# One-hot operands made two batches ahead instead of one, in a graph network's count building

## The chip, the core and the metric

The kernel runs on one core of a Trainium2 chip. The metric is the device time of one execution in microseconds (us). Five engines work side by side, each through its own instructions in their program order, and wait for each other by semaphores: PE (TensorE, matrix products; its weight loads are shown as an engine of their own, PEld), DVE (VectorE), ACT (ScalarE), POOL (GpSimd, which here asks for rows by indirect transfers) and SP (SyncE, which only starts transfers).

## What is computed

The reference normalises x (6250 nodes by 256 channels), and then runs four layers of a graph network over 100000 edges that are sorted by destination. A layer adds to each node the sum of its neighbours' rows and puts the result through a small network of three matrices:

```python
h = jnp.maximum(_layernorm(x, axis=-1), 0.0)
def agg(h):
    return jax.ops.segment_sum(h[src], dst, num_segments=N)
for l in range(NL - 1):
    h = x + agg(x)
    h = jax.nn.relu(h @ W1s[l] + b1s[l])
    h = jax.nn.relu(h @ W2s[l] + b2s[l])
    x = h @ W3s[l] + b3s[l]
h = x + agg(x)
h = jax.nn.relu(h @ cW1 + cb1)
h = jax.nn.relu(h @ cW2 + cb2)
return h @ cW3 + cb3
```

The result is x plus what this returns. All of it is float32.

## The kernel before

The 6250 nodes are 49 blocks of 128. For 31 of them the neighbour sum is a dense product: a matrix of edge counts (how many edges go from each of the 6250 sources to each of the 128 destinations of the block, uint8) times the node rows. For the others the rows are gathered by indirect transfers on POOL (L1427) and summed with matmuls against a small one-hot (`hot`, L1450; matmuls L1466; the sum is added to the node's own row by L1486 and L1495).

**Building the counts.** The count matrices are made once, during the first layer, by the generator `build` (L1092 to L1131). A block is two halves of 64 destinations. A half is 16 groups of 4 destinations, each with up to 128 edges that lie on the partitions. A batch is 4 groups. For a batch DVE writes two one-hot tiles in bf16: `lo`, 128 edges by 4x128 (which of the 128 rows of a source block), and `hi`, 128 edges by 4x196 (which of 49 source blocks and which of 4 destinations). Both come from L1073, called by `low_hot` and `high_hot`; each kind has two buffers. A matmul of `lo` by `hi` (L1114, 196 columns) gives the counts of one group in PSUM. Two groups share a PSUM tile `bp` (three buffers), and are converted to uint8 into `at`: the first pair of a batch by ACT (L1122), the second by DVE (L1124). In the first 24 steps (a step is one pair, two steps are a batch) ACT does both. When a block is whole, DVE adds the identity (L1128, the node's own row) and SP stores the matrix (L1129) for the later layers. `pair` (L1068, ACT) spreads the indices of a half for DVE; it is made one half ahead.

**What runs around it.** In the first layer PE goes through units: a unit is up to 4 matmuls of 512 columns (L1642) of a node block's product, whose left side `a` ACT converts from uint8 (L1602). Before each unit, `tick` issues what has come due: `un` (L1654, the product's two halves added), the MLP of finished blocks (L1526 transposes, L1276 and L1333 matmuls, `zz` at L1341), the gathered sums (L1466). Then `product_by_node` takes steps from `build` until a goal for this unit is reached: in most units one batch, in about one in four none, now and then one and a half. Then come the unit's own matmuls. Ahead of all that, 12 batches are built back to back (L1760 to L1765).

All engines run their instructions in the order in which these calls are made (`manual_schedule`, L1001). On DVE the order around batch k is: what `tick` issued before it, `lo` of k+1, `hi` of k+1, the conversion of k's second pair (L1124); if a block has ended, L1128.

Of the kernel before, what the change touches and what calls it, by code (L numbers as in the profile page):

```python
# [396 lines left out]
def sorted_edges(  # L397
# [55 lines left out]
    BATCH = 4  # L453
# [547 lines left out]
    with tc.manual_schedule():  # L1001
# [61 lines left out]
        def pair(hots, k):  # L1063

            if k < len(batches):
                s = batches[k][0]
                pairs[s] = hots.tile([P, 2, GSUB, 2], BF16, name="pairs", bufs=3)
                nc.scalar.copy(pairs[s], clT[:, :, :, s - S0, None].to_broadcast([P, 2, GSUB, 2]))  # L1068

        def one_hot(o, values, which, n):  # L1070

            shape = [P, BATCH, n // 2, 2]
            nc.vector.tensor_tensor(  # L1073
                o.rearrange("p q (n t) -> p q n t", t=2),
                values.rearrange("p (n t) -> p n t", t=2)[:, None, :, :].to_broadcast(shape),
                which[:, :, None, :].to_broadcast(shape), OP.is_equal)

        def low_hot(hots, k):
            if k < len(batches):
                s, q0 = batches[k]  # L1080
                lo = hots.tile([P, BATCH, P], BF16, name="lo", bufs=2)
                one_hot(lo, lanes, pairs[s][:, 1, q0:q0 + BATCH, :], P)
                hot[k] = [lo]

        def high_hot(hots, k):
            if k < len(batches):
                s, q0 = batches[k]
                hi = hots.tile([P, BATCH, HW], BF16, name="hi", bufs=2)
                one_hot(hi, cols, pairs[s][:, 0, q0:q0 + BATCH, :], HW)
                hot[k].append(hi)  # L1090

        def build(hots, ats, ps_b):  # L1092


            each = GSUB // BATCH
            pair(hots, 0)
            low_hot(hots, 0)
            high_hot(hots, 0)
            step = 0
            for k, (s, q0) in enumerate(batches):  # L1100
                b, half = divmod(s, 2)
                if half == 0 and q0 == 0:
                    at = counts[b] = ats.tile([P, NT, P], U8, name="at", bufs=3)
                lo, hi = hot.pop(k)
                if q0 == 0:
                    pair(hots, k + each)
                for q in range(0, BATCH, 2):
                    if q == 0:
                        low_hot(hots, k + 1)
                    elif q == 2:  # L1110
                        high_hot(hots, k + 1)
                    bp = ps_b.tile([P, W], F32, name="bp")
                    for m in range(2):
                        mm = nc.tensor.matmul(bp[:, m * HW:(m + 1) * HW], lo[:, q + m, :],  # L1114
                                              hi[:, q + m, :], start=True, stop=True)
                    passed(BUILD, mm)
                    d = half * 64 + (q0 + q) * GD
                    o = at[:, :, d:d + 2 * GD].rearrange("p h (i d) -> p h i d", i=2)
                    v = bp[:, :2 * HW].rearrange("p (i h d) -> p h i d", i=2, d=GD)
                    step += 1  # L1120
                    if step % 2 or step <= 2 * PRE:
                        nc.scalar.copy(o, v)  # L1122
                    else:
                        nc.vector.tensor_copy(o, v)  # L1124
                    if half and q0 + q + 2 == GSUB:
                        p, i = place_of[b]
                        own = at[:, b, :]
                        nc.vector.tensor_tensor(own, own, ident, OP.add)  # L1128
                        nc.sync.dma_start(out=mats[p][:, :, i, :],  # L1129
                                          in_=at.rearrange("p (k h) d -> p k (h d)", h=CH))  # L1130
                    yield  # L1131
# [449 lines left out]
        def passed(t, ins=None):  # L1581

            clock[0] += t
            if ins is not None:
                paced[:] = [ins.ins.name]
                for g in layers:
                    g.flow()
# [160 lines left out]
        with tc.tile_pool(name="hots", bufs=1) as hots, tc.tile_pool(  # L1748
            name="ats", bufs=1
        ) as ats, tc.tile_pool(name="rings", bufs=AHEAD + 2) as rings, tc.tile_pool(  # L1750
            name="gath", bufs=24
        ) as gath, tc.tile_pool(
            name="ps_a", bufs=2, space=PSUM
        ) as ps_a, tc.tile_pool(name="ps_b", bufs=3, space=PSUM) as ps_b:
            begun = {0: clock[0]}
            rings.tile([P, 192], U8, name="align", bufs=1)
            layers[0].begin()
            layers[0].send(8)
            beside = build(hots, ats, ps_b)
            while now[0] < PRE:  # L1760
                for _ in range(2):
                    next(beside)
                    built[0] += 1
                tick(layers[0])
                layers[0].advance()  # L1765
            later(1, lambda: later(2, lambda bad=verdict(): judge(bad)))
            for team in teams:
                product_of_team(*team, ps_a, beside, team == teams[-1])
            assert next(beside, None) is None and built[0] == total
# [73 lines left out]
```

## Time and profile before

| | us |
|---|---|
| median of 3 runs | 2105.08 (2103.89 to 2105.66) |
| the profiled execution | 2104.15 |
| its span, first to last instruction | 2102.4 |
| counts built (first to last L1114) | 116.6 to 638.0 |

| engine | busy us | share of the span |
|---|---|---|
| PE | 2031.7 | 97% |
| PEld | 1501.4 | 71% |
| POOL | 1441.1 | 69% |
| DVE | 933.8 | 44% |
| ACT | 879.7 | 42% |

In the profile's groups of instructions the number after the bar is the busy time, then the mean duration of one, then the idle time of that engine just before them and what ended it. In the view of waits a row is "who waits, for whom: total us, times, longest". A timeline row begins with the start and the duration in us; the bracket is the idle time before it and what ended it. Durations of neighbours on one engine overlap a little, so the step from start to start is what an instruction costs in a full queue.

### The profile page before, as it was taken

How to read it: one execution, taken by the hardware profiler on the slowest of the kernel's cores; microseconds unless marked ns; L12 is line 12 of the kernel's file. 1: busy time of each engine (PE TensorE's matmuls, PEld its weight loads, DVE VectorE, ACT ScalarE, POOL GpSimd, SP SyncE). 2: the span in 40 equal slices, each digit the busy share in tenths (PEclk: the TensorE clock that was granted, in tenths of full speed). 3: DMA queues.
4: the chain of work that ended last, by engine and by line, in shares of the span. 5: the costliest groups of instructions: out<-in, count | busy, mean ns of one | idle time of the engine just before them, and what ended most of it. 6: DMA issues, size and time to landing. Idle time of an engine off the chain costs nothing. (4 is left out here: it accounts for less than half of the span.)

```text
span 2102.4 us, 33308 instructions
## 1 busy us (share of the span) xinstructions
PE 2031.7 (97%) x12117; PEld 1501.4 (71%) x12117; DVE 933.8 (44%) x2108; ACT 879.7 (42%) x1799; POOL 1441.1 (69%) x1450
## 2 busy tenths in 40 slices
PE   6889999999999999999999999999999999999997
PEld 4667666666667777777777777777777777777775
DVE  5987767767673422222233322222224333333333
ACT  5866656556555523322333432323333433323331
POOL 3747777777774377777777377777777377777773
PEclk9999999999999999999999999999999999999999
DMA  5544545545554654545556555555456455656554
GB/s 166 171 136 137 158 150 154 157 150 153 155 153 145 212 163 146 169 152 179 155 174 196 186 165 149 172 159 179 147 171 202 161 179 156 196 174 206 169 171 129
DMA packets 184324, 346.92 MB, mean 165 GB/s; under 512 B 32030, under 2 KB 118080, under 8 KB 184150
## 3 DMA queue, kind: packets, MB, share of 16 engines
q0 software_dynamic: 68144, 183.13, 29.9%
q1 hardware_dynamic: 114078, 159.72, 23.1%
q8 instruction: 97, 1.59, 0.3%
q10 hardware_dynamic: 1928, 1.85, 0.3%
q14 instruction: 77, 0.63, 0.1%
HBM read 286.50 MB, written 58.07 MB: 164 GB/s over the span
## 5 line engine op out<-in xcount | busy, mean ns | idle before, releaser
L1427 POOL DMA_INDIRECT rows<-table,idx x1377 | 1381.2, 1003 | 587.5 <-issue 225.4
L1720 PE MATMUL agg<-a,XY 128*128 128x512 f32 x4116 | 976.6, 394 | 1.9 <-DVE clT L1654 1.9
L1720 PEld LDWEIGHTS agg<-a,XY 128*128 128x128 f32 x4116 | 765.2, 188 | 190.1 <-issue 32.4
L1618 ACT CAST a<-at 128x512 fp32r<-128x512 uint8 (+1 forms) x549 | 332.7, 616 | 633.2 <-PE agg L1720 591.3
L1618 DVE CAST a<-at 128x512 fp32r<-128x512 uint8 (+1 forms) x550 | 251.0, 458 | 522.4 <-PE agg L1720 476.0
L1642 PE MATMUL agg<-XY,a 128*128 128x512 f32 x1519 | 420.9, 410 | 1.7 <-ACT a L1602 1.0
L1642 PEld LDWEIGHTS agg<-XY,a 128*128 128x128 f32 x1519 | 268.3, 189 | 54.2 <-issue 9.2
L1466 PE MATMUL sums<-rows,hot 128*32 128x256 f32 x3726 | 233.4, 381 | 8.7 <-DMA rows<-table,idx 8.5
L1122 ACT CAST at<-bp 128x392 uint8<-128x392 f32 x260 | 125.0, 489 | 188.8 <-PE bp L1114 182.6
L1466 PEld LDWEIGHTS sums<-rows,hot 128*32 128x32 f32 x3726 | 118.5, 109 | 117.1 <-issue 27.6
L1602 ACT CAST a<-at 128x512 fp32r<-128x512 uint8 (+2 forms) x362 | 197.5, 575 | 4.7 <-PE agg L1642 4.7
L1124 DVE CAST at<-bp 128x392 uint8<-128x392 f32 x236 | 132.8, 563 | 133.5 <-PE bp L1114 132.7
L1495 DVE TENSOR_TENSOR u<-u,sums 128x256 f32<-128x256 f32 x81 | 33.9, 419 | 265.3 <-PE agg L1720 241.9
L1114 PE MATMUL bp<-hi,lo 128*128 128x196 bf16 x992 | 129.5, 251 | 16.9 <-DVE hi L1073 16.1
L1073 DVE TENSOR_TENSOR hi<-cols,pairs 128x784 bf16<-128x784 bf16 x248 | 139.1, 561 | 0.0
L1333 PE MATMUL ps<-w,h 128*128 128x256 f32 x588 | 135.1, 382 | 1.4 <-ACT h L1279 0.9
L1276 PE MATMUL ps<-h,w 128*128 128x512 f32 (+3 forms) x332 | 133.7, 545 | 2.0 <-DVE zz L1317 1.7
L1114 PEld LDWEIGHTS <-lo 128*128 128x128 bf16 x992 | 72.8, 98 | 87.7 <-DVE hi L1073 37.3
L1333 PEld LDWEIGHTS ps<-w,h 128*128 128x128 f32 x588 | 112.4, 192 | 18.7 <-ACT h L1279 1.3
L1073 DVE TENSOR_TENSOR lo<-lanes,pairs 128x512 bf16<-128x512 bf16 x248 | 103.6, 418 | 0.2 <-issue 0.2
L1530 ACT ACTIVATE h<-ps,bias 128x256 f32<-128x256 f32 (+1 forms) x116 | 47.5, 464 | 134.1 <-PE ps L1526 134.1
L1341 DVE TENSOR_TENSOR zz<-ps,w 128x512 f32<-128x512 f32 (+1 forms) x75 | 50.2, 678 | 117.1 <-PE ps L1333 117.1
(173 smaller groups left out, 959.0 us busy)
## 6 DMA issues: line engine op xcount, KB each, us to landing
at<-mat SPq DMA_DIRECT2D x152, 448.0 KB
mat<-at SPq DMA_DIRECT2D x31, 784.0 KB
rows<-table,idx POOLq DMA_INDIRECT x1377
table<-zz SPq DMA_DIRECT2D x72, 256.0 KB
back<-table SPq DMA_DIRECT2D x99, 128.0 KB
xs<-in_x_dram SPq DMA_DIRECT2D x8, 768.0 KB
table<-zs SPq DMA_DIRECT2D x12, 512.0 KB
out_dram<-zz SPq DMA_DIRECT2D x24, 256.0 KB
```

What stands on the lines that cost most here:

```text
L1073: nc.vector.tensor_tensor(o.rearrange("p q (n t) -> p q n t", t=2), values.rearrange("p (n t) -> p n t", t=2)[:, None, :, :].to_broadcast( ...
L1114: mm = nc.tensor.matmul(bp[:, m * HW:(m + 1) * HW], lo[:, q + m, :], hi[:, q + m, :], start=True, stop=True)
L1122: nc.scalar.copy(o, v)
L1124: nc.vector.tensor_copy(o, v)
L1276: mm = nc.tensor.matmul(ps[:mp, :w], weights[l][0][:, c, i * P:i * P + mp], h1[:, c, :w], start=(c == 0), stop=(c == KC - 1))
L1333: mm = nc.tensor.matmul(o, h2[0][:, c, nodes], w3[:, c, :], start=(c == 0), stop=(c == KC - 1))
L1427: got = nc.gpsimd.indirect_dma_start(out=t, out_offset=None, in_=tables[self.l][:, :], in_offset=bass.IndirectOffsetOnAxis(ap=idx[:, o:o + ...
L1466: nc.tensor.matmul(self.sums[m * Q:(m + 1) * Q, :C], self.hot[:, c - min(rounds), m, :], self.rows[g, c + 4 * m], start=(c == ROUNDS[0][0] ...
L1602: nc.scalar.copy(a[:, i * m * P:(i + 1) * m * P].rearrange("p (j d) -> p j d", j=m), counts[b][:, j:j + m, :])
L1618: cast(o, at[:, :, d:d + m * P])
L1642: mm = nc.tensor.matmul(agg, a[:, d:d + P], XY[:, j, :], start=(j == 0), stop=(j == NT - 1))
L1720: mm = nc.tensor.matmul(agg[c][:, :w], XY[:, j, o:o + P], a[:, :w], start=(at == 0 and half == 0), stop=(at == NT - 1 and half == 1))
```

## The change

The first two one-hots of each kind are made ahead of the loop. In the loop, the making of `lo` and `hi` for the next batch is taken from the places ahead of the two pairs of a batch; in its stead both one-hots for the batch after the next are made behind the conversion of the second pair, when the batch has been used up. Buffers, operations and their number stay.

```diff
             each = GSUB // BATCH
             pair(hots, 0)
-            low_hot(hots, 0)
-            high_hot(hots, 0)
+            for k in range(2):
+                low_hot(hots, k)
+                high_hot(hots, k)
             step = 0
...
                 for q in range(0, BATCH, 2):
-                    if q == 0:
-                        low_hot(hots, k + 1)
-                    elif q == 2:
-                        high_hot(hots, k + 1)
                     bp = ps_b.tile([P, W], F32, name="bp")
...
                         nc.scalar.copy(o, v)
                     else:
                         nc.vector.tensor_copy(o, v)
+                    if q + 2 == BATCH:
+                        low_hot(hots, k + 2)
+                        high_hot(hots, k + 2)
                     if half and q0 + q + 2 == GSUB:
                         p, i = place_of[b]
                         own = at[:, b, :]
```

## Prediction

> **What bounds the kernel now.** I read the page first, then the waits of the weight loads in the stretch in which counts are built, then timelines at the longest waits.
>
> ```profile
> span 2102.4 us, 33308 instructions
> PE 2031.7 (97%) x12117; PEld 1501.4 (71%) x12117; DVE 933.8 (44%) x2108; ACT 879.7 (42%) x1799; POOL 1441.1 (69%) x1450
> ...
> L1114 PE MATMUL bp<-hi,lo 128*128 128x196 bf16 x992 | 129.5, 251 | 16.9 <-DVE hi L1073 16.1
> L1073 DVE TENSOR_TENSOR hi<-cols,pairs 128x784 bf16<-128x784 bf16 x248 | 139.1, 561 | 0.0
> ```
>
> PE is the bound. The largest idle time ahead of any group of its matmuls is that of the counting matmuls, 16.9 us, of which 16.1 wait for `hi`. That is what the change can touch, and the shown idle time is not all of it, since a matmul's end is modelled. The weight loads tell it better:
>
> ```profile
> 127.00:640.00 513.00, 499.10 (x3388) 351.37 (x3387) 371.44 (x843) 307.97 (x695) 369.70 (x366) 0.99 0.50 149
> ```
>
> ```profile
> PEld L1114 <- DVE hi L1073: 31.4, 60, 1.5
> PEld L1114 <- DVE at L1124: 18.6, 68, 0.3
> ...
> PEld L1114 <- DVE zz L1341: 0.5, 2, 0.3
> ```
>
> The first row is the stretch of 513 us: busy time and instructions of PE, PEld, DVE, ACT and POOL. A load ahead of a batch idles 0.27 us even where nothing is late (18.6/68), while the product's matmuls ahead of it run out. The 60 loads that waited for `hi` idle 31.4, so 31.4 - 60x0.27 = 15.2 us are lost there. Batch by batch, counting the excess over 0.27 of the late ones, I get 15.4 in 28 waits. Before 127 us, in the 12 batches that are built back to back:
>
> ```profile
> PE bp L1114 <- DVE hi L1073: 4.5, 11, 1.1
> ```
>
> **What the change does to the order.** Call X what DVE has to do between the conversion of batch k and the first one-hot of k+2. Before, DVE's order is: conversion k, X, `lo` k+2, `hi` k+2, conversion k+1. After, it is: conversion k, `lo` k+2, `hi` k+2, X, conversion k+1. The one-hots pass X, and nothing else moves: each conversion has the same work ahead of it as before. Where X is empty, nothing changes. The new place needs no new wait: the buffers of k are free when k's last matmul has ended, and the conversion just ahead has waited for that matmul. (With half batches `lo` and `hi` both move ahead too.) X is `hot`, `un`, `zz`, `u`, L1128: 0.2 to 1.7 us.
>
> **A wait that goes whole.**
>
> ```profile
> 278.80 0.57 DVE L1124 CAST at<-bp 128x392 uint8<-128x392 f32 x1 [6.90 <-PE bp L1114]
> 279.46 0.29 DVE L1128 TENSOR_TENSOR at<-at,ident 128x128 uint8<-128x128 uint8 x1
> 279.67 1.28 DVE L1341 TENSOR_TENSOR zz<-ps,w 128x512 f32<-128x512 f32 x2
> 280.87 0.41 DVE L1495 TENSOR_TENSOR u<-u,sums 128x256 f32<-128x256 f32 x1
> 281.20 0.42 DVE L1073 TENSOR_TENSOR lo<-lanes,pairs 128x512 bf16<-128x512 bf16 x1
> 281.54 0.56 DVE L1073 TENSOR_TENSOR hi<-cols,pairs 128x784 bf16<-128x784 bf16 x1
> ```
>
> ```profile
> 282.15 0.11 PEld L1114 LDWEIGHTS <-lo 128*128 128x128 bf16 x2 [1.40 <-DVE hi L1073]
> ```
>
> DVE had idled 6.90 us, and when the matmuls of a batch let it go, X (1.74 us, 279.46 to 281.20) stood ahead of the one-hots. PE lost 1.40 - 0.27 = 1.13. With the one-hots directly behind the conversion (which holds DVE some 0.48 us, 278.80 to 279.28), `hi` ends at 279.28 + 0.34 + 0.56 = 280.18; the load could go at 282.15 - 1.13 = 281.02. Nothing is lost there, and an MLP on PE follows, so the 1.13 us stay.
>
> **A wait that only moves on.**
>
> ```profile
> 513.93 0.56 DVE L1124 CAST at<-bp 128x392 uint8<-128x392 f32 x1
> 514.60 0.29 DVE L1128 TENSOR_TENSOR at<-at,ident 128x128 uint8<-128x128 uint8 x1
> 514.81 0.95 DVE L1450 TENSOR_TENSOR hot<-colf,rel 128x768 f32<-128x768 f32 x1
> 515.68 0.41 DVE L1654 TENSOR_TENSOR un<-un,agg 128x256 f32<-128x256 f32 x1
> 516.01 0.42 DVE L1073 TENSOR_TENSOR lo<-lanes,pairs 128x512 bf16<-128x512 bf16 x1
> 516.35 0.56 DVE L1073 TENSOR_TENSOR hi<-cols,pairs 128x784 bf16<-128x784 bf16 x1
> 516.82 0.56 DVE L1124 CAST at<-bp 128x392 uint8<-128x392 f32 x1
> 517.30 0.42 DVE L1073 TENSOR_TENSOR lo<-lanes,pairs 128x512 bf16<-128x512 bf16 x1
> ```
>
> ```profile
> 516.96 0.28 PEld L1114 LDWEIGHTS <-lo 128*128 128x128 bf16 x4 [1.21 <-DVE hi L1073]
> 518.27 0.28 PEld L1114 LDWEIGHTS <-lo 128*128 128x128 bf16 x4 [0.27 <-DVE hi L1073]
> ```
>
> A unit with a batch takes PE 1.31 us (516.96 to 518.27), and DVE needs 0.81 for the two one-hots (516.01 to 516.82) and 0.48 for a conversion: 1.29. In such a run DVE has no slack, so X is a debt. The wait here is 1.21 - 0.27 = 0.94. After the change `hi` is ready at 514.41 + 0.90 = 515.31, and the batch goes at 516.96 - 0.94 = 516.02. But then X (0.21 + 0.87 + 0.33 = 1.41) runs from 515.22 to 516.63, the conversion to 517.11, and the next `hi` ends at 518.01, while PE wants it at 516.02 + 1.31 = 517.33. With 0.06 from `hi` to load PE waits 0.74: only 0.20 of 0.94 is kept. A debt is paid off only where PE has something else: a unit without a batch, the MLP, a gathered sum.
>
> **The sum.** So for each wait: what is kept is the wait, less what the same DVE work makes later batches of the cluster late. I went through DVE's 843 instructions of the stretch in this way, with steps from start to start, each conversion 0.56 us behind its batch's first load at the earliest. In the order of before this gives 14.9 us of waits (the trace: 15.4), so it holds to 0.6. In the new order 4.9 are left. By cluster, start of each, wait now > left:
>
> - go whole: 211 (0.23), 282 (1.13), 328 (0.24), 355 (0.55), 375 (0.56), 408 (0.44), 440 (0.34), 444 (0.56), 561 (0.62), 608 (1.40), 630 (0.48): 6.5 > 0
> - go in part: 165 (1.04 > 0.35), 262 (0.90 > 0.44), 314 (1.14 > 0.55), 421 (0.81 > 0.41), 517 (0.94 > 0.76), 579 (2.26 > 0.54): 7.1 > 3.05
> - stays: 494 (1.71 > 1.76); the last 0.1 is at 199.
>
> Kept: 14.9 - 4.9 = 10.0 by the walk, 10.5 against the trace's waits; I take 10.0.
>
> At the start, 11 waits: ten are 0.3, because a batch there takes PE 0.51 and DVE 0.81, with no X between; they stay. The eleventh has one:
>
> ```profile
> 123.57 0.29 DVE L1128 TENSOR_TENSOR at<-at,ident 128x128 uint8<-128x128 uint8 x1 [0.54 <-ACT at L1122]
> ```
>
> ```profile
> 124.73 0.51 PE L1114 MATMUL bp<-hi,lo 128*128 128x196 bf16 x4 [1.13 <-DVE hi L1073]
> ```
>
> ```profile
> 125.11 2.66 ACT L1122 CAST at<-bp 128x392 uint8<-128x392 f32 x6 [0.66 <-PE bp L1114]
> ```
>
> Here `lo` stood behind L1128, which waited 0.54 for ACT. The one-hots pass it, and PE goes on. But ACT, which does all conversions here and then the first `a` for which PE waits, idled only 0.66 of it, so between 0 and 0.66 comes through; I take 0.6, as nothing else holds ACT there.
>
> **What is moved back.** X starts up to 0.81 us later. In the stretch no load except those of L1114 waited for X (`zz`: 0.5 us in 2, the usual 0.27 each), and what reads it comes units later: a table store, a transpose, the next gathered sum. L1128 only holds up SP's store and casts of a block whose units come later. I take 0; the bound is 134 pieces of X (the stretch's `hot`, `un`, `zz`, `u` and L1128) by 0.81 = 109 us if PE always waited at once for X, and not below 0. ACT, POOL and SP issue what they did.
>
> Against its own time: 2104.15 - 10.0 - 0.6 = 2093.55. That execution was 0.93 below the median; on the median's scale 2105.08 - 10.6 = **2094.5**.
>
> **The rivals.**
>
> *All of it comes back.* If DVE finds room for X in idle time that my walk doesn't see, all goes: 15.4 + 0.7 = 16.1, so 2089.0. For: DVE is busy 371 of 513 us. Against: the run at 517, where it has 0.02 per batch to spare.
>
> *DVE is the bound in the clusters*, and waits mostly move on, as at 517, where 0.20 of 0.94 stays: 15.4 x 0.21 = 3.3, so 2101.8, inside what can be told from no change (0.2%, about 4 us for this kernel). For: the cluster at 494. Against: most long waits come after DVE has idled, with MLP work on PE behind.
>
> *It does nothing*: if X were mostly recorded behind the one-hots already, the time stays, 2105. Against: the two timelines.
>
> *Slower: the gathers.* POOL builds its indirect transfers beside the one-hots:
>
> ```profile
> L1427 POOL DMA_INDIRECT rows<-table,idx x8: 957/1180/1320, 115.8 to 126.1; - x8
> ```
>
> ```profile
> L1427 POOL DMA_INDIRECT rows<-table,idx x366: 947/953/1850, 126.1 to 639.0; - x183
> ```
>
> ```profile
> POOL rows L1427 <- PE bp L1114: 41.4, 91, 2.8
> POOL rows L1427 <- PE agg L1642: 37.0, 68, 10.0
> ```
>
> Where one-hots run back to back a gather takes 1.18 us (median), over the stretch mostly 0.95 (mean 369.70/366 = 1.01). POOL's slack is what it waits for PE: 78.4 in 159 waits, less some 0.3 each that is there anyway, 31 us. If the new places put every gather beside a one-hot, 366 x 0.17 = 62 us come on, 31 beyond the slack; PE would wait for rows from a mean of 1.01 + 31/366 = 1.09 us on, and the time would be 2105.08 - 10.6 + 31 = 2125. Against: there are as many one-hots as before, in almost the same places. The Trainium skill, "SBUF — State Buffer", section "Who interferes with whom", says that a VectorE operation with two SBUF inputs contends with GpSimd's reads through a shared port, and that issue order decides who blocks. The trace agrees as far as 0.95 against 1.18 goes; by that rule the loss could as well fall on DVE, but the one-hots take 0.42 and 0.56 everywhere, so here it is POOL that stretches.
>
> **How the numbers follow.** The forecast has 0.66, all of it 0.15, DVE the bound 0.10, nothing 0.03, the gathers 0.06. Range: from 2088 (all of it, less 1 for the scatter between runs of +-0.9) to 2102 (DVE the bound); left out are the last two and some of the edges. The likeliest alone: 2092 to 2097. Faster by over 0.2%: 0.66 + 0.15 and a little of the third, 0.82; within: 0.12; slower: 0.06.
>
> **What would show it.** In the changed profile L1073's pair follows L1124 directly; at the place of the 282 us wait the load of L1114 has no excess; the waits of L1114's loads for `hi` in the stretch have an excess near 5 us, most in the run near 494 and its like; the last L1114 ends near 627 in place of 638, and the layers after it take as long as before. Wrong would be: an excess over 10 us; new waits of PE for `zz`, `u`, `un` or `hot`; a gather mean above 1.09 with L1466 waiting for rows; or a gain in the first layer that a later stage gives back.

## The result and the profile after

The changed kernel took 2092.72 us (median of 4 runs, 2091.27 to 2094.35), the kernel before 2105.37 in the same sessions: a ratio of 0.9943, 95% interval 0.9930 to 0.9957, 12.65 us less. The forecast was 2094.5, with 2088 to 2102 as its range. The profiled execution took 2093.95 with a span of 2092.2; its counting matmuls have moved from L1114 to L1111, and DVE's conversion from L1124 to L1121, by the lines that the change took out.

From the page of the changed kernel:

```profile
span 2092.2 us, 33309 instructions
PE 2032.2 (97%) x12117; PEld 1504.3 (72%) x12117; DVE 931.1 (45%) x2108; ACT 880.3 (42%) x1799; POOL 1445.3 (69%) x1450
...
L1111 PE MATMUL bp<-hi,lo 128*128 128x196 bf16 x992 | 132.0, 254 | 6.5 <-DVE hi L1073 5.7
```

DVE makes as many instructions as before (2108), and the busy times of PE, DVE and ACT differ by less than 3 us; the idle time ahead of the counting matmuls is 6.5 us in place of 16.9. The waits of the weight loads, from 127 to 640 us:

```profile
PEld L1111 <- DVE at L1121: 20.0, 73, 0.3
PEld L1111 <- DVE hi L1073: 18.6, 50, 1.4
...
PEld L1111 <- DVE at L1128: 1.3, 5, 0.3
PEld L1111 <- DVE zz L1341: 0.8, 3, 0.3
```

For `hi`, 18.6 us in 50 waits, less 0.27 each, is 5.1 lost, where it was 15.2. Below, "excess" means the same, load by load: idle time over 0.27 us, summed over the loads of the 13th batch and later that idled over 0.30 for a one-hot. It is 15.6 us in 29 loads before, and 5.6 in 13 after. The waits that end with X (`zz`, L1128) are no longer than the usual 0.27.

The place of the 1.13 us wait, first DVE and then the loads:

```profile
277.62 0.57 DVE L1121 CAST at<-bp 128x392 uint8<-128x392 f32 x1 [6.89 <-PE bp L1111]
278.10 0.41 DVE L1073 TENSOR_TENSOR lo<-lanes,pairs 128x512 bf16<-128x512 bf16 x1
278.43 0.56 DVE L1073 TENSOR_TENSOR hi<-cols,pairs 128x784 bf16<-128x784 bf16 x1
278.91 0.28 DVE L1128 TENSOR_TENSOR at<-at,ident 128x128 uint8<-128x128 uint8 x1
279.11 1.28 DVE L1341 TENSOR_TENSOR zz<-ps,w 128x512 f32<-128x512 f32 x2
```

```profile
279.29 0.46 PEld L1111 LDWEIGHTS <-lo 128*128 128x128 bf16 x6 [0.26 <-DVE at L1128]
```

The pair stands directly behind the conversion, X behind it, and the load is not late. The row merges the four loads of one batch and the first two of the next, the late ones of before, which now follow without a gap. The place where a wait only moves on, DVE's X and then the loads:

```profile
509.85 0.95 DVE L1450 TENSOR_TENSOR hot<-colf,rel 128x768 f32<-128x768 f32 x1
510.72 0.41 DVE L1654 TENSOR_TENSOR un<-un,agg 128x256 f32<-128x256 f32 x1
511.05 0.56 DVE L1121 CAST at<-bp 128x392 uint8<-128x392 f32 x1
511.53 0.41 DVE L1073 TENSOR_TENSOR lo<-lanes,pairs 128x512 bf16<-128x512 bf16 x1
511.86 0.56 DVE L1073 TENSOR_TENSOR hi<-cols,pairs 128x784 bf16<-128x784 bf16 x1
```

```profile
510.44 0.29 PEld L1111 LDWEIGHTS <-lo 128*128 128x128 bf16 x4 [0.28 <-issue]
512.47 0.28 PEld L1111 LDWEIGHTS <-lo 128*128 128x128 bf16 x4 [0.99 <-DVE hi L1073]
```

The batch at 510.44 is in time, and the next one idles 0.99, an excess of 0.72 where 0.74 was worked out.

**Where the 10.2 us of span went.** The loads of the counting matmuls, in the kernel before and the changed one:

```profile
L1114 PEld LDWEIGHTS <-lo x992: 95/98/152, 116.2 to 637.9; 128*128 128x128 bf16 x199
```

```profile
L1111 PEld LDWEIGHTS <-lo x992: 95/98/152, 116.2 to 628.7; 128*128 128x128 bf16 x199
```

They start at the same time and end 9.2 us earlier. The other 1.0 is no part of the change: 1.6 came with a dip of TensorE's granted clock (0.91 on the mean of 680 to 700 us), which of these two executions only the one of before has, and 0.8 was lost again near 2001, where rows for a gathered sum came late.

### The profile page after: what moved, and what is told of

It is laid out like the page before. It is cut to its first block, busy times and chain, and to the rows that moved or that the text cites. A ratio compares the mean times of both kernels' runs of the same rounds, so it can differ in the third digit from the quotient of the medians.

```text
span 2092.2 us, 33309 instructions
## 1 busy us (share of the span) xinstructions
PE 2032.2 (97%) x12117; PEld 1504.3 (72%) x12117; DVE 931.1 (45%) x2108; ACT 880.3 (42%) x1799; POOL 1445.3 (69%) x1450
## 3 DMA queue, kind: packets, MB, share of 16 engines
q10 hardware_dynamic: 1928, 1.85, 0.3%
## 5 line engine op out<-in xcount | busy, mean ns | idle before, releaser
L1642 PE MATMUL agg<-XY,a 128*128 128x512 f32 x1519 | 421.0, 410 | 1.7 <-ACT a L1602 1.0
L1642 PEld LDWEIGHTS agg<-XY,a 128*128 128x128 f32 x1519 | 268.3, 189 | 54.1 <-issue 9.2
L1121 DVE CAST at<-bp 128x392 uint8<-128x392 f32 x236 | 133.2, 565 | 134.6 <-PE bp L1111 133.8
L1111 PE MATMUL bp<-hi,lo 128*128 128x196 bf16 x992 | 132.0, 254 | 6.5 <-DVE hi L1073 5.7
L1111 PEld LDWEIGHTS <-lo 128*128 128x128 bf16 x992 | 74.0, 99 | 76.9 <-issue 24.5
```

Source lines behind the costliest of these rows:

```text
L1642: mm = nc.tensor.matmul(agg, a[:, d:d + P], XY[:, j, :], start=(j == 0), stop=(j == NT - 1))
```

## The experiments

Each is set against the kernel before of its own session: 2103.45 us for `hi` alone, the two with `hot` twice and the changed kernel with ACT; 2103.69 for the two with 21 row buffers, the one ahead and the first from batch 12; 2104.02 for the last four rows. "Walk" is the excess that the prediction's way through DVE's rows gives for each order.

| kernel | median us | against before | excess us (loads) | walk us |
|---|---|---|---|---|
| before | 2105.37 | | 15.6 (29) | 14.9 |
| changed | 2092.72 | -12.65 | 5.6 (13) | 4.9 |
| only `hi` two ahead | 2098.46 | -5.0 | 12.8 (23) | 12.1 |
| before, `hot` twice | 2118.48 | +15.0 | 30.6 (34) | 28.0 |
| changed, `hot` twice | 2104.71 | +1.3 | 16.0 (23) | 14.3 |
| changed, ACT converts 3 of 4 | 2086.98 | -16.5 | 1.4 (4) | 1.1 |
| changed, 21 row buffers | 2095.19 | -8.5 | 5.5 (13) | |
| three ahead, 21 row buffers | 2089.18 | -14.5 | 0.0 | 0.0 |
| one ahead, behind the conversion | 2207.9 | +104.2 | 113.7 (156) | 116.1 |
| changed from batch 12 on | 2095.88 | -7.8 | 5.5 (13) | |
| changed, again | 2091.27 | -12.75 | 5.5 (13) | 4.9 |
| changed from batch 12 on, again | 2094.39 | -9.6 | 5.5 (13) | |
| before, ACT converts 3 of 4 | 2099.04 | -5.0 | 10.9 (23) | 9.0 |
| three ahead, ACT converts 3 of 4 | 2089.85 | -14.2 | 0.0 | 0.4 |

**Only one of the two operands.**

```diff
             low_hot(hots, 0)
-            high_hot(hots, 0)
+            for k in range(2):
+                high_hot(hots, k)
...
                     if q == 0:
                         low_hot(hots, k + 1)
-                    elif q == 2:
-                        high_hot(hots, k + 1)
...
+                    if q + 2 == BATCH:
+                        high_hot(hots, k + 2)
```

> Edit: only the hi one-hot is made two batches ahead behind the conversion; lo keeps its place of before, ahead of the next batch and behind X. Theory (the pair passes X, and PE needs both): lo still stands behind X, so only the 0.48 us that hi takes is gained at a late batch and most of it becomes a wait further on; going through the DVE rows of before in this order leaves 12.1 us of 14.9 us of waits, a gain of 2.8 us over before, 2102.6 us, and the loads now wait for lo in place of hi. Rival (the late operand is hi, as the profile names it in 60 waits against 13 for lo): nearly the whole gain of the change, 10 to 12.6 us, 2093 to 2095 us.

Ratio 0.9979 (0.9969 to 0.9990). The excess falls by 2.8 us as the theory has it; the time, by the ratio, by 4.4 (2.1 to 6.5), an interval that holds the theory's 2.8 and not the rival's 10. The loads from 127 to 640 us:

```profile
PEld L1113 <- DVE lo L1073: 26.7, 52, 1.5
```

The profile now names `lo`. It had named `hi` only because `hi` came last: both stood behind X.

**X made longer, in both kernels.**

```diff
-                nc.vector.tensor_tensor(
-                    self.hot,
+                for _ in range(2 if self.l == 0 else 1):
+                    nc.vector.tensor_tensor(
+                        self.hot,
...
```

> Edit: in the kernel before, DVE writes the small one-hot of the gathered sums (hot, a piece of X, 0.87 us of DVE) twice in the first layer, 21 or so more instructions. Theory (X stands ahead of the one-hots and a late batch is lost PE time): 13.2 us slower than before, 2118.6 us, by the same walk through the DVE rows. Rival (DVE has idle time enough, 142 of 513 us, and X hides in it): under 3 us slower. Rival (DVE is the bound of the stage): the whole 21 x 0.87 = 18.3 us, 2123.7 us.

> Edit: the same doubled hot in the changed kernel. Theory: the one-hots pass X, but X remains a debt in runs of batches without slack: 9.4 us slower than the changed kernel, 2102.1 us, less than the same edit costs in the kernel before (13.2). Rival (with the change X is off the path): under 3 us. Rival (DVE is the bound of the stage): 18.3 us, 2111.0 us.

The same DVE work costs the kernel before 15.0 us (ratio 1.0073, 1.0056 to 1.0090) and the changed one 12.0 against its 2092.72, or 13.4 against the 2091.27 of a later session. By excess, which is not blurred by the scatter between runs, it is 15.0 and 10.5. Loads of before and of the changed kernel with the longer X, from 127 to 640 us:

```profile
PEld L1114 <- DVE hi L1073: 46.6, 64, 2.5
```

```profile
PEld L1111 <- DVE hi L1073: 32.1, 61, 2.4
```

So X is on the path in both, and the change makes it cheaper, not free. The 3 us of work that hides is far outside. The 18.3 us of a stage bound by DVE alone is told apart by the excess (15.0 and 10.5); the time of the kernel before alone, with 11.8 to 18.9 us as its interval, would leave room for it. The walk had 13.2 and 9.4: the sign and the order right, both 1 to 2 us low by the excess.

**DVE relieved, with the change and without.** The same one-line edit was put into both kernels:

```diff
-                    if step % 2 or step <= 2 * PRE:
+                    if step % 4 or step <= 2 * PRE:
                         nc.scalar.copy(o, v)
```

> Edit: the changed kernel with ACT converting three of four pairs instead of two, so DVE has 0.48 us less in every second batch. Theory (what is left, 5.5 us of excess at 13 loads, is DVE without slack in runs of batches): 3.7 us faster than the changed kernel, 2089.0 us, excess about 1 us. Rival (what is left is the distance of two batches, not DVE's rate): no change, 2092.7 us. Rival (ACT, 313 us busy of 513 and in order with the casts for PE, becomes late): slower than 2095 us with PE waiting for a.

> Edit: the kernel before with ACT converting three of four pairs; the one-hots stay behind X. Theory (two causes that add: X stands ahead of the one-hots, and DVE has no slack to pay it off; relief of DVE alone leaves the first): 5.9 us faster than the kernel before, about 9 us of excess left at the loads, against 1.4 us left with both edits. Rival (DVE's rate is the whole cause): all 15 us gone, 2089 us, as with both edits.

With the change it is 2086.98 (ratio to before 0.9920, 0.9903 to 0.9937), the fastest kernel of all here: 5.7 us below the changed kernel, or 4.3 below the 2091.27 of its later session, where 3.7 was expected. Without the change it gains 5.0 (ratio 0.9975, 0.9966 to 0.9984), where 5.9 was expected. The loads of the two:

```profile
PEld L1111 <- DVE lo L1073: 13.5, 50, 0.3
PEld L1111 <- DVE hi L1073: 9.1, 30, 1.0
```

```profile
PEld L1114 <- DVE hi L1073: 25.0, 53, 1.5
```

The excess tells the two causes apart: 15.6 as it was, 10.9 with DVE relieved, 5.6 with the one-hots ahead of X, 1.4 with both. ACT did not become late: PE waited once for `a`, 1.2 us, as in the changed kernel (1.0).

**More distance.** A third buffer of each kind needs 2592 bytes of every partition (4x128 and 4x196 values of 2 bytes). Three row buffers of 1 KB each are given up for it, so 21 are left, in a control too.

```diff
-            name="gath", bufs=24
+            name="gath", bufs=21
```

> Edit: the changed kernel with 21 row buffers for the gathers of the first layer instead of 24, to make room for the next run; its control. Theory and rivals: a visit takes 17 rows, and 4 more can be asked for ahead, so within 1.5 us of the changed kernel, 2092.7 us; if rows come late PE waits for them at L1466 and it is slower by the sum of those waits.

The control came out 2.5 us above the changed kernel, more than the 1.5 expected, at the same excess for one-hots. Fewer row buffers do bring waits for rows. The loads of the gathered sums from 127 to 640 us, in the changed kernel and in the control:

```profile
PEld sums L1466 <- DMA rows<-table,idx: 2.1, 5, 0.8
```

```profile
PEld sums L1466 <- DMA rows<-table,idx: 4.2, 5, 1.4
```

That is 2.1 us more, about the size of the difference, in one execution of each. The next kernel is set against this control.

```diff
-                lo = hots.tile([P, BATCH, P], BF16, name="lo", bufs=2)
+                lo = hots.tile([P, BATCH, P], BF16, name="lo", bufs=3)
...
-                hi = hots.tile([P, BATCH, HW], BF16, name="hi", bufs=2)
+                hi = hots.tile([P, BATCH, HW], BF16, name="hi", bufs=3)
...
-            for k in range(2):
+            for k in range(3):
...
-                        low_hot(hots, k + 2)
-                        high_hot(hots, k + 2)
+                        low_hot(hots, k + 3)
+                        high_hot(hots, k + 3)
```

> Edit: the control with three buffers of each one-hot, made three batches ahead. Theory (the waits left in the changed kernel are debts of X that come due one or two batches later, and a batch more of distance lets them be paid where PE has other work): the walk through the DVE rows leaves 0.0 of 4.9 us of waits, so 4.9 us faster than the control, about 2087.8 us. Rival (DVE's rate is the bound in these runs, distance doesn't help): the time of the control, excess about 5.5 us as in the changed kernel.

The third batch removes the whole excess and 6.0 us of the control's time (2089.18 against 2095.19; the times lie at 2088.82 to 2096.13 and 2094.36 to 2097.0). So in the runs without slack distance does help: DVE finds room later, when PE is at an MLP or a gathered sum. Its profiled execution, at 2096.13 the slowest of its four, waited still longer for rows (6.2 us at these loads), once like this:

```profile
316.67 1.70 PE L1466 MATMUL sums<-rows,hot 128*32 128x256 f32 x25 [1.76 <-DMA rows<-table,idx]
```

**Both remedies together.** The last two edits in one kernel.

> Edit: three buffers and three batches ahead (21 row buffers for the gathers) with ACT converting three of four pairs. Theory: nearly no wait for one-hots is left in either edit alone, so together no more than each: excess under 0.5 us, 2086 to 2089 us. Rival (they add): 2082 us. Rival (fewer row buffers bring waits for rows): slower than 2090 us with those waits at L1466.

They don't add: ratio 0.9935 (0.9921 to 0.9948), and no excess, of which three batches ahead alone had left none. At 2089.85 us it lies just above the 2086 to 2089 expected, and above the kernel that only relieves DVE (2086.98). That kernel has 24 row buffers, and the 21 show here again: the waits for rows with both remedies, and with ACT's alone:

```profile
PEld sums L1466 <- DMA rows<-table,idx: 6.1, 8, 1.7
```

```profile
PEld sums L1466 <- DMA rows<-table,idx: 1.1, 4, 0.4
```

**The place without the distance.**

```diff
-            for k in range(2):
+            for k in range(1):
...
-                        low_hot(hots, k + 2)
-                        high_hot(hots, k + 2)
+                        low_hot(hots, k + 1)
+                        high_hot(hots, k + 1)
```

> Edit: the changed kernel with the one-hots made only one batch ahead, at the new place behind the conversion. Theory: distance counts, not the place: the next batch waits for the matmuls of the last one, the conversion and both one-hots, 0.56 + 0.48 + 0.90 us against the 1.31 us of a unit: the walk gives 101 us over before, 2206 us. Rival (the gain is the place, one-hots before X): as fast as the changed kernel.

104 us slower in one run. The loads of three batches, one a unit:

```profile
201.24 0.28 PEld L1111 LDWEIGHTS <-lo 128*128 128x128 bf16 x4 [0.26 <-DVE hi L1073]
...
203.22 0.28 PEld L1111 LDWEIGHTS <-lo 128*128 128x128 bf16 x4 [0.94 <-DVE hi L1073]
...
205.20 0.28 PEld L1111 LDWEIGHTS <-lo 128*128 128x128 bf16 x4 [0.95 <-DVE hi L1073]
```

A unit takes 1.98 us (203.22 to 205.20) in place of 1.31: matmuls, conversion and one-hots have become a ring. The new place is only good with the second batch of distance.

**The start.** The first 12 batches get the old order back; the edit against the changed kernel:

```diff
-            for k in range(2):
-                low_hot(hots, k)
-                high_hot(hots, k)
+            low_hot(hots, 0)
+            high_hot(hots, 0)
...
+                    if k < 12 and q == 0:
+                        low_hot(hots, k + 1)
+                    elif k < 12:
+                        high_hot(hots, k + 1)
...
-                    if q + 2 == BATCH:
+                    if k >= 11 and q + 2 == BATCH:
```

> Edit: the changed kernel, but the first 12 batches, which are built back to back, are made one ahead as before. Theory (the start gained nothing: the 1.13 us wait went, but ACT bounds this stretch and TensorE's granted clock fell earlier): within 0.6 us of the changed kernel, 2092.7 us, first product matmul near 128.2 us of the span as in both. Rival (part of the gain, 0.6 us, is from the start): 2093.3 us, and the matmul 0.6 us later. The granted clock from 118 to 130 us is read in every run: if the half clock begins at another time in other runs too, it isn't the change that moves it.

> Edit: none, the changed kernel again, beside the next runs on one chip. Theory and rivals: 0.994 of the kernel before, some 2092.7 us; the scatter between sessions is what the other comparisons must be held against.

> Edit: the changed kernel with the first 12 batches made one ahead as before, again, now beside the changed kernel. Theory (nothing is gained at the start): the time of the changed kernel within 1 us. Rival (the first batches carry a part of the gain): 0.6 to 3 us slower than the changed kernel, as the medians of two sessions had it, 2095.9 against 2092.7 us.

Both times the median came out some 3 us above the changed kernel's (2095.88 against 2092.72, 2094.39 against 2091.27), not within the 0.6 and the 1 us expected, and more than any wait at the start is long. The second pair ran on one chip, and the times overlap (2089.23 to 2095.32 and 2091.49 to 2096.21). The traces say less. The first product matmul of the changed kernel (L1642), and of this one in its second session (L1645 there), in executions in which the granted clock fell at the same time (0.70 and 0.63 from 118 to 121 us, 0.50 from 121 to 130):

```profile
128.15 2.07 PE L1642 MATMUL agg<-XY,a 128*128 128x512 f32 x4 [1.03 <-ACT a L1602]
```

```profile
125.27 1.65 PE L1114 MATMUL bp<-hi,lo 128*128 128x196 bf16 x8 [0.96 <-DVE hi L1073]
...
129.09 1.22 PE L1645 MATMUL agg<-XY,a 128*128 128x512 f32 x2 [1.03 <-ACT a L1605]
```

With the old order the wait for `hi` is back, and the product begins 0.94 us later. At the first load of the 17th batch 0.34 of it is left (137.49 and 137.83 us), and at the last load of the counts nothing (628.7 and 628.4). So the start carries 0.9 at most; why the medians differ by 3 is not settled.

## Why the prediction was right

- **The bound.** PE, late at the counting matmuls for DVE: the shown idle time there fell by 10.4 us, the excess by 10.0, and the stretch ended 9.2 earlier.
- **Order alone.** That the passing of X is what counts is shown by the runs with `hot` twice and with `hi` alone; that the new place needs the second batch of distance, by the run with one batch. Two batches of distance at the old place were not run.
- **The sum.** 10.0 was taken for the stretch (4.9 left of 14.9), and 5.6 of 15.6 were left. That both differences are 10.0 is in part luck, as the walk is 0.7 low on either side. Of the 13 loads still late, 12 are in the clusters named as going in part or staying, and the other is the one at 199. The 494 cluster kept 1.75 in three loads, 1.76 by the walk. The term that was off is the cluster at 579: 0.54 was to be left, and three loads kept 1.4.

```profile
571.45 0.57 DVE L1121 CAST at<-bp 128x392 uint8<-128x392 f32 x1 [2.79 <-PE bp L1111]
571.93 0.43 DVE L1073 TENSOR_TENSOR lo<-lanes,pairs 128x512 bf16<-128x512 bf16 x1
572.28 0.56 DVE L1073 TENSOR_TENSOR hi<-cols,pairs 128x784 bf16<-128x784 bf16 x1
```

```profile
572.89 0.28 PEld L1111 LDWEIGHTS <-lo 128*128 128x128 bf16 x4 [0.62 <-DVE hi L1073]
574.17 0.11 PEld L1111 LDWEIGHTS <-lo 128*128 128x128 bf16 x2 [1.00 <-DVE hi L1073]
```

In the kernel before, the same two loads waited as long:

```profile
579.29 0.28 PEld L1114 LDWEIGHTS <-lo 128*128 128x128 bf16 x4 [0.60 <-DVE hi L1073]
580.57 0.11 PEld L1114 LDWEIGHTS <-lo 128*128 128x128 bf16 x2 [1.00 <-DVE hi L1073]
```

There is no X between conversion and one-hots there, so by the prediction's own rule (where X is empty, nothing changes) these waits (0.33 and 0.73 over 0.27) had to stay; the walk, which left 0.54 in the whole cluster, wrongly let about half of them go. After a gathered sum PE took one and a half batches at once, and then wanted a one-hot that could only begin when the batch before last had been converted. Such a wait was not for this change to remove; three batches ahead removes it.

- **The start.** 0.6 was taken, and no run shows it as such. In the profiled execution nothing had come through at the 17th batch (first load at 137.5 us, 137.4 before; the 9.2 us all come later), with a half clock that came 6 us earlier than in the one of before and lasted 13.7 us in place of 6.8. Against the old order at nearly the same clock it is 0.94 at the first product and 0.34 at the 17th batch.
- **What is moved back** cost nothing that the loads show: the counting loads wait for `zz`, `u`, `un`, `hot` and L1128 for 0.3 at most at a time, and the one wait of another load for `un`, 1.1 us near the end of the stretch, is in the kernel before too.
- **The rivals.** All of it didn't come back (5.6 left). Waits that mostly move on, as with DVE for the bound, were found in the 494 and 517 clusters alone, and three batches ahead removed even these. POOL's gathers took 379.90/371 = 1.02 us on the mean (1.01 before; 1.09 was the point from which they would decide):

```profile
127.00:640.00 513.00, 506.61 (x3428) 357.68 (x3432) 368.53 (x845) 313.21 (x710) 379.90 (x371) 0.99 0.51 154
```

The 0.17 us that this rival put on every gather beside a one-hot is not borne out. In the stretch of the kernel before, the 22 gathers with nine tenths or more of their time beside one-hots took 0.95 us (median; 0.98 at most), and so did the 84 beside none (median 0.95). So what stretches a gather to 1.18 at the start, and whether the shared port does, stays open.

- **The size.** 12.65 against 10.6; the interval of the measured gain is 9.1 to 14.7 us, so the two are not told apart. The waits show 10.0. No run ties the other 2.6 to the change: the two profiled executions of the changed kernel (2093.95 and 2091.27 us) differ by as much, 2.2 of it before the 17th batch, where TensorE's granted clock differed (last section).

## What to carry to other kernels

An operand made ahead on an in-order engine is only as early as the work recorded in front of it: look at what stands between "its buffer is free" and "it is made", and move it past that before adding buffers. The gain is the wait less the debt that the passed work leaves: where that engine has no slack per turn, the wait comes back one turn later, and then less work or one more buffer is the remedy. Either alone left next to nothing here (1.4 and 0.0 us of excess), so there was nothing for both together to gain. The operand that the profile names is the last to arrive, which need not be the only late one.

## What the hardware showed that was not expected

In every profiled execution TensorE's granted clock fell to half (0.50) early in the counts, beginning between 118.8 and 128.3 us of the span. The changed kernel, with the granted clock as the third figure from the end:

```profile
118.00:121.00 3.00, 2.37 (x15) 1.36 (x16) 2.90 (x8) 3.00 (x9) 2.39 (x3) 0.70 0.48 145
121.00:124.00 3.00, 2.61 (x15) 1.38 (x13) 2.84 (x8) 2.87 (x8) 2.39 (x3) 0.50 0.35 93
```

Here the half clock began at 119.2 us (0.70 on the mean of 3 us is 1.8 us at half) and lasted 13.7. In the second session of the same kernel it began at 119.2 too but lasted 3.4, so that the clock was at full speed from 124 us on; there the first load of the 17th batch went at 135.3 us in place of 137.5. So the ten more microseconds of half clock, under which the products began, went with some 2 us of time.

The Trainium skill, "TensorE: Matmul & The Clock Gate", section "What's actually happening", says that the clock is halved after an idle window of about 3.4 us and that the window runs freely, so that its phase differs from run to run. The traces agree with the half (0.50), with the window (these falls lasted 3.41, 6.83 or 13.65 us: one, two or four of it) and with another start in another execution of the same kernel: with the old order in the first 12 batches it began at 125.5 us in one session and at 118.8 in the next. They do not show an idle window: ahead of the fall at 119.2, PE was busy for 1.85 of the 3 us from 115 to 118.
